# Weights of two feed-forward stages and the last attention's keys and values, prepared in steps inside the stage ahead

## The chip, the cores and the metric

The kernel runs on one core of one Trainium2 chip. The metric is the device time of one execution in microseconds (us); the number that counts is the median of repeated runs. The engines are PE (TensorE: matrix products, and transposes done as matrix products), DVE (VectorE), ACT (ScalarE), POOL (GpSimd) and SP (SyncE, which here issues the loads). "PEld" is PE's loading of the fixed operand, which overlaps its products. PSUM, the memory into which PE writes, is handed out in banks; every result has to be copied out of its bank by another engine before the bank can be used again.

## The reference

A network of four pairs of cross-attention and feed-forward stage on x (2048 tokens of 256 numbers), with a context of 1601 rows:

```python
x = x + _L0_xattn_ref(_layernorm(x, axis=-1), ctx_1024, ...)
x = x + _L0_ffn_ref(_layernorm(x, axis=-1), L0_ffn_gate_w, L0_ffn_experts)
x = x + _L1_xattn_ref(_layernorm(x, axis=-1), ctx_1024, mask_BxSxS2_ik0, L1_xattn_Wq, L1_xattn_Wk, L1_xattn_Wv)
x = x + _L1_ffn_ref(_layernorm(x, axis=-1), L1_ffn_fast_b, L1_ffn_w_fc, L1_ffn_w_proj, L1_ffn_u, L1_ffn_v, L1_ffn_gate)
x = x + _L2_xattn_ref(_layernorm(x, axis=-1), ctx_1024, L2_xattn_edge_index, ...)
x = x + _L2_ffn_ref(_layernorm(x, axis=-1), L2_ffn_w_up, L2_ffn_w_down)
x = x + _L3_xattn_ref(_layernorm(x, axis=-1), ctx_1024, ctx_1024, mask_1x1xSxS2_ik0, L3_xattn_Wq, ...)
x = x + _L3_ffn_ref(_layernorm(x, axis=-1), L3_ffn_w1, L3_ffn_b1, L3_ffn_w2, L3_ffn_b2)
```

What matters here are the two ternary feed-forwards. Their weights are turned into -1, 0 and 1 before they are used:

```python
# L1, "bitlinear": one scale for each row; a low-rank product is added to the first layer
scale = clip(mean(abs(w_latent), axis=1, keepdims=True), 1e-05, None)
tern  = clip(round(w_latent / scale), -1.0, 1.0)
h = x @ (tern * scale).T + gate * (x @ v.T @ fast_b.T @ u.T)
return bitlinear(maximum(h, 0.0) ** 2, w_proj)

# L2: one threshold for the whole matrix; the input is divided by its root mean square
alpha = mean(abs(w))
w_t = sign(w) * (abs(w) > 0.5 * alpha)
```

The last attention (L3) has 16 heads of 16 numbers, with a bias on queries, keys, values and output. The masks of L1 and L3 are such that only the last 400 rows of the context count; the kernel finds this out when it runs and then takes the branch described here.

## The kernel before

**Tiling.** x stays on the chip as 16 tiles of 128 tokens. A chunk is 512 tokens, four tiles, so each stage has four chunks (c = 0 to 3). The stages run one after another: attention 0, experts, a branch on what the masks hold, and then, in the branch that is taken, `attention1_tail` (L1, lines 883 to 992), `ffn1` (1028 to 1170), `attention1` (L2, 725 to 881), `ffn2` (1193 to 1279), `attention3_tail` (1500 to 1752) and `ffn3`.

**PSUM.** `banks` (line 88) opens three pools for a stage: two double banks for scores (`psc`), two banks for everything else (`pm`: transposes, projections, sums) and two accumulators (`pa`). A stage closes them at its end. `attention3_tail` opens 3, 1 and 1 for its main part.

**Attentions L1 and L2.** Before the first chunk they transpose their weights, make keys kT (and a rounded copy kb, line 923 in L1) and values v (lines 927 to 931). Then for each chunk come scores (974 to 977 in L1, 851 to 860 in L2), an exponential on ACT, and value products (984, 871) in four accumulations, one for each tile. What the next chunk needs (its norm, its queries q and qb, the maxima for the exponential) is written as a generator, `prepare`, and advanced by `step(nxt, n)` between the scores and between the accumulations: the helper takes n pieces of work from a generator, up to the next `yield`.

**ffn1.** It loads w_fc and w_proj (1 MB each) into raw weight buffers when the function is entered. Within the stage it then prepares: the absolute mean of each row (`scales`, the reduces of line 1054, DVE), the ternary weights (`ternary`, lines 994 to 1000: two DVE instructions, one for each comparison), their transposes in bf16 on PE with copies by ACT (`transpose_up` with 1009 and 1012, `transpose_down` with 1021 and 1025), and the low-rank matrices b4 and vh, vl from u, fast_b and v (1076 to 1104). Only then does the first chunk's norm follow (transposes of line 173, copies xnhi and xnlo of lines 179 and 180), with the low-rank product (1123), and the four chunks.

**ffn2.** The same for w_up and w_down, with one threshold for a matrix (`thresholds`: a reduce on DVE, and a product with ones, line 1214, to sum over partitions). Each chunk then has four pairs of score products (1245), gelu on ACT, a split in two parts (`parts`, 1172 to 1179), squares h * h on DVE (1256) with their sum on POOL (1257), and the down products (`down`, line 1186), two pairs late. At the end of a chunk PE sums the squares (1268) and DVE scales the result and adds it to x.

**attention3_tail.** It loads four weights, and prepares keys and values: transposed and padded weights (`transpose_weight`, lines 205 to 220, and 1574), keys in four groups (1582, 1586), values in four row blocks (1592). Its main part begins with the norm, the projection of the queries (1616 to 1621) and maxima.

**What sets the order.** In the attentions L1 and L2 and in the preparations a scheduler orders the instructions of each engine by their dependencies and the order in which they are written. In ffn1 and ffn2 PE's order is the written one from the start of the main part (`manual_schedule(engines={PE})`), and in the last attention's main part that of all engines. The raw weights of all stages share three buffers (`wraw`, 2048 numbers wide) in turn, so a load starts when the weights three earlier in the turn are no longer needed. All of them are issued by SP, in order.

Of the kernel before, what the change touches and what calls it, by code (L numbers as in the profile page):

```python
# [8 lines left out]
F32 = mybir.dt.float32  # L9
BF16 = mybir.dt.bfloat16  # L10
# [44 lines left out]
class Net:  # L55
# [44 lines left out]
    def psc(self):  # L100
        return self.ps_s.tile([P, 2, 512], F32, tag="s", name="psc")

# [102 lines left out]
    def transpose_weight(self, dst, raw, pad=None):  # L205

        nc = self.nc
        for kc in range(2):
            ps = self.pm()
            for o in range(2):  # L210
                nc.tensor.transpose(
                    ps[:, o * P : (o + 1) * P], raw[:, o, kc * P : (kc + 1) * P], self.ident
                )
            if pad:
                nc.scalar.copy(
                    dst[:, kc, :].rearrange("p (h e) -> p h e", e=32)[:, :, 0:16],
                    ps[:, :D].rearrange("p (h e) -> p h e", e=16),
                )
            else:
                nc.scalar.copy(dst[:, kc, :], ps[:, :D])  # L220

# [503 lines left out]
    def attention1(self, pre, mask=None, bias=False):  # L725
# [5 lines left out]
        with ExitStack() as s:  # L731
# [108 lines left out]
            for c in range(NCH):  # L840
# [25 lines left out]
                for i in range(TPC):  # L866
                    x = self.x[c * TPC + i]
                    acc = self.pa()
                    for kt in range(NKT):
# [5 lines left out]
                        if kt % 6 == 5:  # L875
                            step(nxt, 1)
                    ri = self.small.tile([P, 1], F32, name="ri1")
# [5 lines left out]
    def attention1_tail(self, pre, mask):  # L883
# [5 lines left out]
        with ExitStack() as s:  # L889
# [75 lines left out]
            for c in range(NCH):  # L965
# [14 lines left out]
                for i in range(TPC):  # L980
# [7 lines left out]
                    step(nxt, 1)  # L988
                    ri = self.small.tile([P, 1], F32, name="ri1")
# [12 lines left out]
    def transpose_up(self, dst, t):  # L1002

        nc = self.nc
        for kc in range(2):
            for j in range(2):
# [5 lines left out]
                nc.scalar.copy(dst[:, kc, j * 512 : (j + 1) * 512], ps)  # L1012

    def transpose_down(self, dst, t):

        nc = self.nc
        for f in range(0, 8, 2):
# [7 lines left out]
            nc.scalar.copy(dst[:, f : f + 2, :], ps.rearrange("p (k o) -> p k o", k=2))  # L1025


    def ffn1(self):
# [6 lines left out]
        self.load_rows("L1_ffn_w_proj", F, wpr)  # L1035
        with ExitStack() as s:
            self.banks(s)
            pool = s.enter_context(tc.tile_pool(name="f1", bufs=1))
            tp = s.enter_context(tc.tile_pool(name="f1t", bufs=3))
            hp = s.enter_context(tc.tile_pool(name="f1h", bufs=2))  # L1040
            u = pool.tile([P, NF, R], F32, name="u")
            vv = pool.tile([R, D], F32, name="vv")
            fb = pool.tile([R, R], F32, name="fb")
            gate = pool.tile([R, 1], F32, name="gate")
            nc.sync.dma_start(u, a["L1_ffn_u"].rearrange("(o p) r -> p o r", p=P))
            nc.sync.dma_start(vv, a["L1_ffn_v"])
            nc.sync.dma_start(fb, a["L1_ffn_fast_b"])
            nc.sync.dma_start(gate, a["L1_ffn_gate"].partition_broadcast(R))

            def scales(view, n, cols):  # L1050
                sc = pool.tile([P, n], F32, name=f"sc{n}")
                half = pool.tile([P, n], F32, name=f"half{n}")
                nhalf = pool.tile([P, n], F32, name=f"nhalf{n}")
                nc.vector.tensor_reduce(sc, view, AX.X, ALU.add, apply_absolute_value=True)
                nc.vector.tensor_scalar(sc, sc, 1.0 / cols, 1e-5, ALU.mult, ALU.max)
                nc.vector.tensor_scalar(half, sc, 0.5, None, ALU.mult)
                nc.vector.tensor_scalar(nhalf, sc, -0.5, None, ALU.mult)
                return sc, half, nhalf


            sc1, half, nhalf = scales(wfc, NF, D)
            rs1 = pool.tile([P, NF], F32, name="rs1")
            nc.vector.reciprocal(rs1, sc1)
            tfc = pool.tile([P, NF, D], BF16, name="tfc")
            for o in range(NF):
                self.ternary(tp, tfc[:, o, :], wfc[:, o, :], half[:, o : o + 1], nhalf[:, o : o + 1])
                nc.vector.tensor_scalar(u[:, o, :], u[:, o, :], rs1[:, o : o + 1], None, ALU.mult)
            wfT = pool.tile([P, 2, F], F32R, name="wfT")
            self.transpose_up(wfT, tfc)


            uT = pool.tile([R, F], F32, name="uT")
            b = pool.tile([R, F], F32, name="b")
            bh = pool.tile([R, 2, F], F32R, name="bh")
            b4 = pool.tile([P, F], F32R, name="b4")
            nc.gpsimd.memset(b4.bitcast(F32), 0.0)
            for j in range(2):
                ps = self.pm()
                for i in range(4):
                    nc.tensor.transpose(ps[0:R, i * P : (i + 1) * P], u[:, 4 * j + i, :], self.ident)  # L1080
                nc.scalar.copy(uT[:, j * 512 : (j + 1) * 512], ps[0:R, :])
                ps = self.pm()
                nc.tensor.matmul(ps[0:R, :], lhsT=fb, rhs=uT[:, j * 512 : (j + 1) * 512], start=True, stop=True)
                nc.vector.tensor_scalar(b[:, j * 512 : (j + 1) * 512], ps[0:R, :], gate, None, ALU.mult)
            nc.vector.tensor_copy(bh[:, 0, :], b)
            nc.vector.tensor_tensor(bh[:, 1, :], b, bh[:, 0, :].bitcast(F32), ALU.subtract)
            for k in range(4):
                nc.scalar.copy(b4[32 * k : 32 * k + R, :], bh[:, k % 2, :])

            v4 = pool.tile([P, 2, P], F32, name="v4")  # L1090
            nc.gpsimd.memset(v4, 0.0)
            vh = pool.tile([P, 2, P], F32R, name="vh")
            vl = pool.tile([P, 2, P], F32R, name="vl")
            ps = self.pm()
            for kc in range(2):
                nc.tensor.transpose(ps[:, kc * R : (kc + 1) * R], vv[:, kc * P : (kc + 1) * P], self.ident[:R, :R])
            for k in range(4):
                nc.vector.tensor_copy(
                    v4[:, :, 32 * k : 32 * k + R], ps[:, : 2 * R].rearrange("p (k r) -> p k r", k=2)
                )  # L1100
            nc.vector.tensor_copy(vh, v4)
            nc.vector.tensor_tensor(vl, v4, vh.bitcast(F32), ALU.subtract)
            sc2, half, nhalf = scales(wpr, 2, F)
            tpr = pool.tile([P, 2, F], BF16, name="tpr")
            for o in range(2):
                self.ternary(tp, tpr[:, o, :], wpr[:, o, :], half[:, o : o + 1], nhalf[:, o : o + 1])
            wpT = pool.tile([P, NF, D], F32R, name="wpT")
            self.transpose_down(wpT, tpr)

            scb = pool.tile([P, D], F32, name="scb")  # L1110
            ps = self.pm()
            for o in range(2):
                nc.tensor.transpose(
                    ps[:, o * P : (o + 1) * P], sc2[:, o : o + 1].to_broadcast([P, P]), self.ident
                )
            nc.scalar.copy(scb, ps[:, :D])
# [76 lines left out]
    def ffn2(self):  # L1193
# [7 lines left out]
        self.load_rows("L2_ffn_w_down", F, wdn)  # L1201
        with ExitStack() as s:
            self.banks(s)
            pool = s.enter_context(tc.tile_pool(name="f2", bufs=1))
            tp = s.enter_context(tc.tile_pool(name="f2t", bufs=3))
            hp = s.enter_context(tc.tile_pool(name="f2h", bufs=2))

            def thresholds(view, name):
                part = pool.tile([P, 1], F32, name=f"part{name}")
                half = pool.tile([P, 1], F32, name=f"half{name}")  # L1210
                nhalf = pool.tile([P, 1], F32, name=f"nhalf{name}")
                nc.vector.tensor_reduce(part, view, AX.XY, ALU.add, apply_absolute_value=True)
                ps = self.pm()
                nc.tensor.matmul(ps[:, 0:1], lhsT=self.ones, rhs=part, start=True, stop=True)
                nc.vector.tensor_scalar(half, ps[:, 0:1], 0.5 / (F * D), None, ALU.mult)
                nc.vector.tensor_scalar(nhalf, ps[:, 0:1], -0.5 / (F * D), None, ALU.mult)
                return half, nhalf

            half, nhalf = thresholds(wup, "u")
            tup = pool.tile([P, NF, D], BF16, name="tup")  # L1220
            tflat = tup.rearrange("p o i -> p (o i)")
            for o in range(0, NF, 4):
                self.ternary(tp, tflat[:, o * D : (o + 4) * D], wflat[:, o * D : (o + 4) * D], half, nhalf)
            half, nhalf = thresholds(wdn, "d")
            tdn = pool.tile([P, 2, F], BF16, name="tdn")
            for o in range(2):
                self.ternary(tp, tdn[:, o, :], wdn[:, o, :], half, nhalf)
            wuT = pool.tile([P, 2, F], F32R, name="wuT")
            self.transpose_up(wuT, tup)
            wdT = pool.tile([P, NF, D], F32R, name="wdT")  # L1230
# [4 lines left out]
            for c in range(NCH):  # L1235
# [4 lines left out]
                for f in range(0, NF, 2):  # L1240
# [20 lines left out]
                    if f == 2 and c + 1 < NCH:  # L1261
                        nxt = self.norm(c + 1, rms=True, split=hp)
# [603 lines left out]
```

## Time and profile before

| | us |
|---|---|
| median of 3 runs (2095.49 to 2098.01) | 2097.05 |
| the profiled execution | 2097.01 |
| its span, first to last instruction | 2095.2 |
| PE busy in it | 1866.5 (89%) |
| DVE busy | 1115.3 (53%) |
| ACT busy | 822.2 (39%) |
| POOL busy | 686.9 (33%) |

The mean granted clock of PE is 0.951 of full speed. The stages of the branch lie in the span as follows (us from its start): L1's attention from about 988 to 1101.7, ffn1 to about 1235, L2's attention to 1516.1, ffn2 to 1643.2, the last attention to about 1979, ffn3 to 2095.2.

In the rows of the profile, "PE pa L984" is an instruction of PE that writes a tile called pa and comes from line 984. A row of the chain of waits has its start and its length; where two rows don't touch, the time between them belongs to pieces of the chain that aren't shown. A busy PE isn't PE at its peak, since the ends of its products are modelled.

### The profile page before, as it was taken

To read this page: it belongs to the slowest core of one execution; us is meant where nothing else is said; L and a number is where in the kernel's file an instruction comes from. 1 tells how busy PE (TensorE), PEld (TensorE's weight loads), DVE (VectorE), ACT (ScalarE), POOL (GpSimd) and SP (SyncE) were. 2 spreads that over 40 slices of the span, in tenths; PEclk is the share of its full clock that TensorE was granted. 3 is DMA by queue.
4 is the path that set the end of the run, shared out by engine and by line. 5 is a ranking of instruction groups with operands and counts; after the bars stand their busy time and mean duration, and the time that the engine had idled before them with its cause. 6 is when DMAs were issued, how large, how long until landed. Compare 5 with 4: busy or idle time off the path is not lost.

```text
span 2095.2 us, 22283 instructions
## 1 busy us (share of the span) xinstructions
PE 1866.5 (89%) x8523; PEld 924.4 (44%) x8533; DVE 1115.3 (53%) x2170; ACT 822.2 (39%) x1121; POOL 686.9 (33%) x469
## 2 busy tenths in 40 slices
PE   7789999999999899886995899999968888988899
PEld 3233333333333443332453664555556522333487
DVE  4665565655644377778436643222176467766400
ACT  4554434434434247740113431111143256555432
POOL 1168878867868300028000120000033201111210
PEclk9799999999999799998997999999978889999999
DMA  8830000000000000001001000000000000000361
GB/s 285 280 100 1 1 1 1 1 1 0 1 1 1 1 1 1 1 1 63 8 0 43 1 23 1 0 1 0 0 1 1 6 1 1 1 1 1 130 194 61
DMA packets 39698, 63.49 MB, mean 30 GB/s; under 512 B 5133, under 2 KB 32158, under 8 KB 39582
## 3 DMA queue, kind: packets, MB, share of 16 engines
q1 hardware_dynamic: 37776, 60.33, 8.8%
q10 hardware_dynamic: 1806, 1.64, 0.2%
q8 instruction: 69, 1.13, 0.2%
q14 instruction: 47, 0.39, 0.1%
HBM read 59.87 MB, written 2.10 MB: 30 GB/s over the span
## 4 chain that ended last, share of the span: by engine, by line
PE 65%; DVE 15%; ACT 7%; issue 5%; POOL 5%; DMA 3%; SPq 0%; ACTq 0%; POOLq 0%; DVEq 0%
PE pa L468 7%; PE psc L456 5%; PE psc L851 5%; PE pa L871 4%; PE psc L1649 3%; DVE mp L381 3%; PE psc L1787 3%; PE pa L561 3%; PE pa L1798 3%; DVE ri L418 2%; ACT p L1656 2%; PE psc L454 2%; PE pm L1699 2%; PE pm L1616 2%; PE pm L376 2%
## 5 line engine op out<-in xcount | busy, mean ns | idle before, releaser
L477 POOL TENSOR_TENSOR sp<-sp,p 128x1024 f32<-128x1024 f32 (+1 forms) x176 | 418.7, 2379 | 56.9 <-ACT p L461 46.4
L381 DVE TENSOR_REDUCE mp<-pm 128x1 f32<-128x512 f32 x384 | 242.7, 679 | 160.2 <-PE pm L376 159.5
L461 ACT ACTIVATE p<-psc 128x1024 f32<-128x1024 f32 (+1 forms) x208 | 212.7, 1023 | 260.9 <-PE psc L456 162.2
L456 PE MATMUL psc<-qT,kT 64*128 64x512 f32 (+1 forms) x832 | 219.8, 591 | 0.0
L468 PE MATMUL pa<-p,v 128*64 128x512 f32 (+1 forms) x832 | 203.6, 611 | 0.0
L1656 ACT ACTIVATE p<-psc 100x1024 f32<-100x1024 f32 x128 | 124.0, 1021 | 76.1 <-PE psc L1649 72.5
L1635 DVE TENSOR_REDUCE ms<-psc 128x2 bf16<-128x800 f32 x128 | 122.7, 981 | 43.8 <-PE psc L1631 41.9
L144 POOL TENSOR_SCALAR rstd<-mv 128x4 f32<-128x4 f32 x32 | 8.7, 272 | 365.2 <-DVE mv L140 357.9
L376 PE MATMUL pm<-kb,qb 64*128 64x512 bf16 x384 | 100.3, 391 | 26.6 <-DVE mp L381 24.9
L468 PEld LDWEIGHTS pa<-p,v 128*64 128x64 f32 (+1 forms) x832 | 51.0, 137 | 132.4 <-issue 129.4
L851 PE MATMUL psc<-q,kT 128*128 128x512 f32 (+1 forms) x208 | 102.2, 610 | 0.0
L702 POOL TENSOR_SCALAR done<-done,g 128x256 f32<-128x256 f32 x32 | 32.4, 1013 | 205.3 <-DVE g L696 205.3
L657 DVE SCALAR_TENSOR_TENSOR ge<-bc,g,after 128x128 bf16<-128x128 f32 (+8 forms) x128 | 79.4, 648 | 33.7 <-ACT seen L642 25.3
L1691 POOL TENSOR_TENSOR attn<-o,ri 128x512 f32<-128x512 f32 x16 | 20.3, 1270 | 229.3 <-DVE ri L1689 208.1
L456 PEld LDWEIGHTS psc<-qT,kT 64*128 64x128 f32 (+1 forms) x832 | 85.4, 185 | 19.6 <-issue 6.3
L871 PE MATMUL pa<-v,p 128*128 128x257 f32 (+1 forms) x416 | 93.9, 381 | 0.2
L864 ACT ACTIVATE p<-psc 128x1024 f32<-128x1024 f32 (+1 forms) x28 | 26.9, 962 | 168.2 <-PE psc L860 168.2
L636 PE MATMUL psc<-ge,pick 128*8 128x512 bf16 (+3 forms) x332 | 75.5, 344 | 19.5 <-DVE ge L657 10.6
L454 PE MATMUL psc<-sh,negz 64*128 64x512 bf16 (+1 forms) x416 | 87.0, 384 | 3.3 <-ACT sh L403 3.2
L151 DVE TENSOR_SCALAR xn<-x,mv,rstd 128x256 f32<-128x256 f32 x128 | 51.6, 460 | 68.1 <-PE pm L173 66.8
L824 DVE TENSOR_REDUCE mp<-pm 128x1 f32<-128x512 f32 x64 | 34.3, 570 | 99.9 <-PE pm L819 90.6
L642 ACT ACTIVATE seen<-ge 128x1152 bf16<-128x1152 bf16 (+6 forms) x56 | 83.2, 1486 | 6.7 <-DVE ge L662 5.8
(354 smaller groups left out, 3382.3 us busy)
## 6 DMA issues: line engine op xcount, KB each, us to landing
w<-in_L_ffn_w_dram SPq DMA_DIRECT2D x16, 1024.0 KB, 7.0
head<-in_mask_BxSxS_ik_dram SPq DMA_DIRECT2D x16, 600.5 KB, 4.0
head<-in_mask_1x1xSxS_ik_dram SPq DMA_DIRECT2D x16, 600.5 KB, 4.2
tail<-in_mask_BxSxS_ik_dram SPq DMA_DIRECT2D x16, 200.0 KB, 4.1
tail<-in_mask_1x1xSxS_ik_dram SPq DMA_DIRECT2D x16, 200.0 KB, 4.1
x<-in_x_dram SPq DMA_DIRECT2D x16, 128.0 KB, 3.4
w_e<-in_L_ffn_experts_dram SPq DMA_DIRECT2D x2, 1024.0 KB, 7.4
out_dram<-y SPq DMA_DIRECT2D x16, 128.0 KB, 2.5
```

The source lines that it names most:

```text
L376: nc.tensor.matmul(pair[j][:, :wd], lhsT=qb[h, i * P : (i + 1) * P], rhs=kb[h, hp, k0 : k0 + wd], start=True, stop=True,)
L381: nc.vector.tensor_reduce(mp[:, i, j, n : n + 1], pair[j][:, :wd], AX.X, ALU.max)
L454: nc.tensor.matmul(sc[:r, j, :], lhsT=negz[h, :r], rhs=sh[h, :], start=True, stop=False)
L456: nc.tensor.matmul(sc[:r, j, :], lhsT=kT[h, hp, kt * P : kt * P + r], rhs=q[h, :], start=False, stop=True,)
L461: nc.scalar.activation(p[:r], sc[:r], AF.Exp, scale=DH**-0.5)
L468: nc.tensor.matmul(acc[h, :], lhsT=v[:r, kt, hp * P + h.start : hp * P + h.stop], rhs=p[:r, j, :], start=kt == 0, stop=kt == NKT - 1,)
L477: nc.gpsimd.tensor_tensor(sums[:r], sums[:r], p[:r], ALU.add)
L642: nc.scalar.activation(seen[:, (t + 1) * P :], ge[:, (t + 1) * P :], AF.Copy, accum_out=far[:, t, e : e + 1])
L851: nc.tensor.matmul(sc[:r, j, :], lhsT=kT[:, kc, ks], rhs=q[:, kc, :], start=kc == 0, stop=False)
L871: nc.tensor.matmul(acc[:, : D + 1], lhsT=p[:r, kt, i * P : (i + 1) * P], rhs=v[:r, kt, :], start=kt == 0, stop=kt == NKT - 1,)
L1635: nc.vector.tensor_reduce(ms[u % 2][:, i, 64 * k + DH : 64 * k + 64 : 32], ps[:, :, :NTAIL], AX.X, ALU.max)
L1656: nc.scalar.activation(p[:TR], sc[k][:TR], AF.Exp, scale=DH**-0.5)
```

## The change

`ffn1`, `ffn2` and `attention3_tail` are each split in two. The first half becomes a generator: `ffn1_weights`, `ffn2_weights` and `attention3_keys` hold the loads and all the preparation, with a `yield` after each piece. The second half is the main part. The generators are advanced within the stage ahead: `attention1_tail` takes two steps after each of its 16 accumulations, `attention1` (L2) one, and `ffn2` two after each of its 16 pairs of score products. `finish` runs what is left. The tiles of a preparation live in pools that are opened before those of the stage ahead, and the ternary helper has its own pool of two buffers (f1l, f2l). The values' weight wvT has a tile of its own.

The loads of ffn1's weights come ahead of those of L1's on SP, those of ffn2's ahead of L2's, and those of L3's at the start of ffn2; so the turn of the raw buffers changes too. The transposes' helpers yield after each evacuation.

```diff
+    def finish(self, steps):
+        with ExitStack() as s:
+            self.banks(s)
+            drain(steps)
...
-    def attention1(self, pre, mask=None, bias=False):
+    def attention1(self, pre, mask=None, bias=False, beside=None):
...
+                    step(beside, 1)
                     ri = self.small.tile([P, 1], F32, name="ri1")
...
-    def attention1_tail(self, pre, mask):
+    def attention1_tail(self, pre, mask, beside=None):
...
                     step(nxt, 1)
+                    step(beside, 2)
...
                 nc.scalar.copy(dst[:, kc, j * 512 : (j + 1) * 512], ps)
+                yield
...
-    def ffn1(self):
+    def ffn1_weights(self, s):
...
+        pool = s.enter_context(tc.tile_pool(name="f1", bufs=1))
+        tp = s.enter_context(tc.tile_pool(name="f1l", bufs=2))
+        u = pool.tile([P, NF, R], F32, name="u")
...
+        nc.sync.dma_start(u, a["L1_ffn_u"].rearrange("(o p) r -> p o r", p=P))
...
+        yield
...
+        for o in range(NF):
+            self.ternary(tp, tfc[:, o, :], wfc[:, o, :], half[:, o : o + 1], nhalf[:, o : o + 1])
+            nc.vector.tensor_scalar(u[:, o, :], u[:, o, :], rs1[:, o : o + 1], None, ALU.mult)
+            if o % 2:
+                yield
+        wfT = pool.tile([P, 2, F], F32R, name="wfT")
+        yield from self.transpose_up(wfT, tfc)
...
+        self.f1 = wfT, wpT, b4, vh, vl, sc1, scb
+
+    def ffn1(self):
+        tc, nc = self.tc, self.nc
+        NF = 8
+        wfT, wpT, b4, vh, vl, sc1, scb = self.f1
...
-    def ffn2(self):
+    def ffn2_weights(self, s):
...
+        half, nhalf = thresholds(wup, "u")
...
+        for o in range(0, NF, 4):
+            yield
+            self.ternary(tp, tflat[:, o * D : (o + 4) * D], wflat[:, o * D : (o + 4) * D], half, nhalf)
+        half, nhalf = thresholds(wdn, "d")
+        yield
...
+    def ffn2(self, beside=None):
...
                     if f == 2 and c + 1 < NCH:
                         nxt = self.norm(c + 1, rms=True, split=hp)
+                    step(beside, 2)
...
-    def attention3_tail(self, mask):
+    def attention3_keys(self, mask, s):
...
+        kv = s.enter_context(tc.tile_pool(name="kv3", bufs=1))
+        yield
...
+        wvT = kv.tile([P, 2, D], F32, name="wvT")
...
+        for w, n, pad in ((wkT, "Wk", True), (wqT, "Wq", True), (wvT, "Wv", None)):
+            yield from self.transpose_weight_steps(w, raw[n], pad)
...
+        for g in range(G):
+            ps = self.pm()
...
+            nc.scalar.activation(kT[:, g, :], ps[:, :NTAIL], AF.Identity, bias=kbias[:, g : g + 1])
+            nc.vector.tensor_copy(kb[:, g, :], kT[:, g, :])
+            yield
+        for kt in range(TK):
+            ps = self.pm()
...
+            yield
+        self.k3 = spread, qbias, bo, wqT, woT, kT, kb, v, ms
...
-        net.attention1_tail("L1_xattn", masks[0])
-        net.ffn1()
-        net.attention1("L2_xattn", bias=True)
-        net.ffn2()
-        net.attention3_tail(masks[1])
+        with ExitStack() as s1:
+            later = net.ffn1_weights(s1)
+            step(later, 1)
+            net.attention1_tail("L1_xattn", masks[0], later)
+            net.finish(later)
+            net.ffn1()
+        with ExitStack() as s2:
+            later = net.ffn2_weights(s2)
+            step(later, 1)
+            net.attention1("L2_xattn", bias=True, beside=later)
+            net.finish(later)
+            with ExitStack() as s3:
+                later = net.attention3_keys(masks[1], s3)
+                step(later, 1)
+                net.ffn2(later)
+                net.finish(later)
+                net.attention3_tail()
         net.ffn3()
```

The other branch, which isn't taken, runs the same halves one after the other.

## The prediction

> **What bounds the kernel now.** I read the stage sums first (busy time of each engine in a stretch), then the chain of waits at each of the three places from which the change takes work, then the list of waits in the second FFN. The columns of a stretch are its length, then PE, PEld, DVE, ACT and POOL busy with counts, the granted clock, DMA share and GB/s.
>
> ```profile
> 1101.70:1129.50 27.80, 12.17 (x48) 4.70 (x48) 20.39 (x51) 9.71 (x15) 3.29 (x4) 0.55 0.27 79
> 1516.10:1533.10 17.00, 5.47 (x37) 3.98 (x37) 14.75 (x19) 4.00 (x8) 4.78 (x5) 0.64 0.00 1
> 1643.20:1665.20 22.00, 20.52 (x70) 11.59 (x70) 5.80 (x22) 6.95 (x14) 3.82 (x5) 0.83 0.02 0
> ```
>
> These are the preparations of ffn1, of ffn2 and of the last attention. They are of two kinds. In the first two PE idles and DVE works; in the third PE itself is busy for 20.5 of 22 us, so that work isn't waiting, it is matrix work that must be done somewhere. The stages ahead of them, which are to take the work:
>
> ```profile
> 992.00:1101.70 109.70, 106.35 (x360) 55.60 (x360) 49.91 (x144) 18.20 (x27) 8.86 (x14) 0.95 0.04 15
> 1267.00:1516.00 249.00, 244.78 (x863) 136.81 (x871) 62.34 (x149) 37.25 (x50) 9.90 (x16) 1.00 0.00 0
> 1543.00:1644.00 101.00, 78.69 (x445) 69.25 (x444) 67.67 (x87) 35.58 (x51) 40.73 (x26) 0.88 0.01 3
> ```
>
> The two attentions are PE-bound (97% and 98%) with DVE at 46% and 25%: DVE work is free there, PE work is not. ffn2 is bound by no single engine. The chain of waits, last attention block into the first preparation:
>
> ```profile
> 1094.49 7.17 PE pa L984 x32
> 1101.77 2.29 DVE sc L1054
> 1104.53 2.19 DVE sc L1054
> ...
> 1129.54 1.34 PE pm L173 x5
> ```
>
> Its ends give the first hole: 1129.54 - 1101.7 = 27.8 us from the last value product to the transposes of ffn1's first norm. In the same way the second is 1516.08 to 1533.06, 17.0 us, and the third runs from the end of the sum products L1268 (1643.2) to the first maxima L1616 (1665.23), 22.0 us.
>
> How ffn2 waits from 1565 to 1644 (first what waits, then for what, total us, times, longest):
>
> ```profile
> POOL sq L1257 <- DVE h L1256: 24.4, 5, 9.9
> PE pm L1268 <- POOL sq L1257: 10.2, 3, 3.8
> PE pa L1186 <- DVE rlo L1178: 3.5, 3, 2.4
> ```
>
> A chunk takes 27 us, with PE busy for some 21 and DVE for some 19; its end is a chain DVE, POOL (2.35 us for each sq), PE, so extra DVE or ordered PE work is partly paid there.
>
> **What the Trainium skill says.** Trace Analysis, section Optimization Strategy: where a kernel has several regimes, interleaving them may pay. The rows above agree for the first two holes (DVE-led preparation beside a PE-bound stage) and less for the third. TensorE: Matmul & The Clock Gate, section What's actually happening: PE falls to half clock after an idle window of about 3.4 us. The granted clock of 0.55 and 0.64 in the first two holes, against 0.95 and 1.00 in the attentions, agrees. The same page, section Architectural detail, calls ACT and DVE strict FIFO; so a DVE instruction that is put early holds all behind it. The trace shows each engine's records in order; no run here tests it otherwise.
>
> **The change, part by part.** The profiled execution took 2097.01 us (span 2095.2), the median is 2097.05; so differences on the span carry over one to one. I give what each hole frees and then what comes back.
>
> *ffn1's weights, into the attention L1.* Freed: 27.8 us; after the last L984 PE goes straight to the norm's transposes. Paid:
> (a) The head of the attention. In the changed order DVE has w_fc's whole chain ahead of the first copy of kb: the reduce 2.29, five small ones about 0.4, eight ternary pairs of 0.345 + 0.476 = 6.6, together 9.3. Before, DVE reached that copy at 998.73, with the statistics of the norm done; so it falls to about 1008. Between the copies of kb, v, xn and qb then lie w_pr's reduce 2.28, its pairs 2 x (0.75 + 1.27) = 4.0 and u's scaling 1.8, in part where DVE idled (3.6 us for v, 3.5 for xn, 2.4 for qb). Those idle times hold about 6 of the 8 us, so 2 us are paid: the head is 11 to 12 us late. PE has nothing else there; it is bare.
> (b) Loads. SP now issues w_fc, w_pr and u ahead of L1's three weights, and u waits for the experts' pool (POOL's last add ends 988.2). I put Wk at about 994.5 and its use before at 989.1, 5.5 us late; it lies under (a), which is longer.
> (c) PE work put into a PE-bound stage: 32 bf16 transposes at 0.086 (the hole shows 0.134 at clock 0.64; scaled to full clock) 2.75, eight of u 1.1 (2.0 at 0.55), fb's products 2.1 (3.8 at 0.55), the rest 0.6: 6.6 us.
> (d) Stalls of PE on the two pm banks: each step evacuates by ACT (0.59 each) and the copies of b take 4.2 on ACT, ahead of which exponentials queue. No row shows this wait; at least 0, at most about 8 (the twelve evacuations one after another at 0.59 plus a wait); I take 3.
> Sum: -27.8 + 11.5 + 6.6 + 3 = -7. Bounds: -12 (head late by 7 only) to -2.
>
> *ffn2's weights, into the attention L2.* Freed: 17.0. Paid: 32 bf16 transposes and two threshold products, 3.2 us of PE in a stage with 4 us of slack in 249; the reduces (2 x 2.3) at about 1237 to 1253 under the transposes of L2's weights: 0; the ternary pairs (two of 0.7 + 1.28 for each matrix, 8 us of DVE) hold up chunk 0's maxima and shift: 2; a DVE copy of L1609 in the first chunk and pm stalls: 1. Sum: -17 + 6.2 = -10.8. Bounds -13 to -7.
>
> *The last attention's keys and values, into ffn2.* Freed: not all 22. After the change PE goes from the sum products to the norm of the last attention, and its transposes take the bank in which the last accumulator lay, which DVE frees only after the update of x (about 3 us later); with transposes, xnT, projection and qb it is some 6 us to the first maxima. Freed: 16. Paid: 20.5 us of PE at clock 0.83, about 14.3 at the clock of a busy ffn2, with two steps after each f, so all 18 within chunk 0 and the start of chunk 1. PE idles in a chunk for about 6 us, so 8 of 14 are bare if nothing else waits. But PE's order is fixed: a step's transposes wait for the bank, ACT's evacuation (0.59) and behind them stand the scores of the next f. I work chunk 0 out as +6.2, chunk 1 as +5.8 (norm of the next chunk behind a step, then L1586's kind of product behind xnlo), chunk 2 as +0.7: 12.7. Sum: -16 + 12.7 = -3. Bounds -9 to +4.
>
> *The rest.* Two small pools (f1l, f2l) and the changed turn of the three weight buffers: each load is issued earlier than its use by over 20 us except (b): 0. ffn3's first weights wait for the last attention's pools, as before: 0, at most 2 either way.
>
> Total: -7 - 10.8 - 3 = about -20 us: 2097 - 20 = 2077.
>
> **The rivals.**
> B, cover is better than I take it. For: DVE at half load in the attentions; PE's 22 us of idle in ffn2 are more than the 14 put in. Against: DVE's order at the head is in the program. Then the head costs 5, the stalls 0, ffn2 pays 5: -27.8 + 5 + 6.6 = -16; -17 + 3.2 = -13.8; -16 + 5 = -11; together -41: 2056.
> C, the gaps are closed but nearly given back: the head late by 16, stalls of 6 in the first attention (+0.5), ffn2's weights -8, and ffn2 longer by 18 (+2): -5.5: 2091. For: the fixed orders. Against: no wait on pm banks in the attentions' lists.
> D, slower. One mechanism, in ffn2: the two pm banks are shared by steps, norm and sums, and PE stands at each of the 18 steps until the one before is evacuated behind that engine's own queue (ACT's gelu of 1 us, DVE's h of 1.1, rlo). At 1.9 us a step ffn2 is 34 us longer and the third part +18, which just cancels the first two; at 2.2 us it is +24 and the kernel 2103. For: DVE and ACT waits in ffn2. Against: PE pm L173 waits there for 3.2 us in all over two times now.
> E, the scheduler leaves the work where it was: 2097. The order of the changed kernel's instructions shows it moved; nearly out.
>
> **How the numbers follow.** A 0.57 (2066 to 2088 by its bounds), B 0.13, C 0.18, D 0.07, E with any cancelling sum 0.05. A measurement can tell about 0.2%, 4.2 us, from no change. Faster: A, B and C, less C's edge, 0.87; same 0.06; slower 0.07. The range that leaves out no more than 2 in 10 goes from B's near half to C: 2057 to 2091.
>
> **What would show it.** After, the chain of waits runs from value products straight into L173's transposes after L1 and L2, with holes under 4 us. The first attention's first scores come 11 to 12 us later than 1010.99 counted from the experts' end; if 5 or less, B. ffn2 from its first scores to its last sum product lasts about 120 us against 108; over 140 is D. PE's busy total falls little (the same matrix work at a better clock), its idle time by about 15 us. The prediction is wrong if the first attention gains nothing, or ffn2 grows by over 25 us.

## The result and the profile after

The changed kernel takes 2074.81 us (median of four runs, 2074.35 to 2080.25); the kernel before took 2097.53 beside it (median of four, 2095.49 to 2101.64). The ratio is 0.9895, with a 95% interval from 0.9873 to 0.9917: 22.7 us less, where 20 were forecast. The profiled execution has a span of 2072.9 us, 22.3 less than before, so the trace accounts for the difference.

First the stages that took the work, in the changed kernel (length, then PE, PEld, DVE, ACT and POOL busy, granted clock, DMA share, GB/s): the head of attention L1, its main part, and ffn2 from its first scores to its last sum product.

```profile
988.50:1020.60 32.10, 18.91 (x53) 10.61 (x54) 29.00 (x87) 4.88 (x11) 5.27 (x9) 0.65 0.37 118
1020.60:1117.00 96.40, 96.07 (x371) 49.45 (x370) 42.74 (x114) 25.45 (x36) 5.06 (x8) 1.00 0.03 9
1510.60:1636.00 125.40, 100.13 (x531) 81.76 (x532) 74.20 (x114) 48.22 (x76) 43.93 (x30) 0.86 0.02 3
```

The same three stretches of the kernel before:

```profile
989.00:1010.80 21.80, 18.16 (x49) 10.46 (x50) 14.48 (x53) 4.87 (x11) 5.18 (x10) 0.70 0.36 128
1010.80:1101.70 90.90, 90.51 (x321) 46.56 (x319) 38.19 (x100) 15.27 (x21) 3.79 (x6) 1.00 0.00 1
1534.90:1643.20 108.30, 85.89 (x473) 74.59 (x473) 73.01 (x98) 42.90 (x64) 41.73 (x27) 0.88 0.01 3
```

Read length against busy. The head of L1 has grown by 10.3 us with PE's work unchanged and DVE's doubled: that is waiting. L1's main part has grown by 5.5 with PE busy for over 99.5% in both: that is work. In ffn2 PE's busy time rose by 14.2, and its idle time (length less busy) didn't fall but rose, from 22.4 to 25.3 us: on balance the work that was put in filled no gap.

Two of the three holes are gone, and the third is shorter. PE's own timeline of the changed kernel (start, length, idle time before it in brackets) at the ends of L1 and of L2, and at the end of ffn2:

```profile
1113.81 3.21 PE L997 MATMUL pa<-v,p 100*128 100x257 f32 x14
1116.86 1.04 PE L179 MATMUL pm<-ident,xn 128*128 128x128 f32 x8
...
1505.74 3.65 PE L882 MATMUL pa<-v,p 128*128 128x257 f32 x16
1509.23 1.04 PE L179 MATMUL pm<-ident,xn 128*128 128x128 f32 x8
...
1632.83 3.57 PE L1315 MATMUL pm<-ones,sq 128*128 128x1 f32 x16 [3.81 <-POOL sq L1303]
1640.03 1.08 PE L179 MATMUL pm<-ident,xn 128*128 128x128 f32 x4 [3.63 <-DVE x L1324]
1643.59 3.78 PE L1672 MATMUL pm<-xnT,w_l3q 128*128 128x512 f32 x4 [0.67 <-ACT xnT L183]
```

After L1 and L2 the value products run straight into ffn's transposes; after ffn2 7.2 us are left between the sums and the first projection, and that projection (four products) takes 3.78 us where it took 1.98.

A ledger from such marks, counted from POOL's last x of the experts (988.3 before, 987.8 after), so that what differs ahead of the change drops out:

| stretch | before | after | difference |
|---|---|---|---|
| head of L1, to its first scores | 22.5 | 32.8 | +10.3 |
| L1, first scores to last value product | 90.5 | 96.0 | +5.5 |
| to ffn1's first low-rank product (first hole) | 31.0 | 2.5 | -28.5 |
| ffn1 and the head of L2, to its first value product | 184.3 | 188.1 | +3.8 |
| L2, first to last value product | 199.1 | 201.8 | +2.7 |
| to ffn2's first scores (second hole) | 19.2 | 1.6 | -17.6 |
| ffn2, first scores to last sum product | 108.3 | 125.4 | +17.1 |
| to the first projection (third hole) | 22.0 | 7.6 | -14.4 |
| last attention and ffn3, to the end | 430.0 | 429.3 | -0.7 |
| sum | 1106.9 | 1085.1 | -21.8 |

Three questions were left for runs: what makes the head late, whether each part pays, and why ffn2 grows by more than the work put into it.

### The profile page after: what moved, and what is told of

Its sections match the earlier page's. It is cut to its first block, busy times and chain, and to the rows that moved or that the text cites. A ratio compares the mean times of both kernels' runs of the same rounds, so it can differ in the third digit from the quotient of the medians.

```text
span 2072.9 us, 22285 instructions
## 1 busy us (share of the span) xinstructions
PE 1853.8 (89%) x8533; PEld 915.1 (44%) x8533; DVE 1114.5 (54%) x2170; ACT 821.5 (40%) x1121; POOL 684.7 (33%) x469
## 5 line engine op out<-in xcount | busy, mean ns | idle before, releaser
L471 ACT ACTIVATE p<-psc 128x1024 f32<-128x1024 f32 (+1 forms) x208 | 212.7, 1023 | 260.5 <-PE psc L466 162.1
L1705 PE MATMUL psc<-q,kT 32*100 32x512 f32 x512 | 75.8, 641 | 10.4 <-ACT p L1712 10.0
L571 PE MATMUL pa<-w_e,xe 128*128 128x512 f32 x160 | 84.7, 655 | 0.0
## 6 DMA issues: line engine op xcount, KB each, us to landing
x<-in_x_dram SPq DMA_DIRECT2D x16, 128.0 KB, 3.6
out_dram<-y SPq DMA_DIRECT2D x16, 128.0 KB, 3.8
```

Of the source, the lines that this page charges most:

```text
L471: nc.scalar.activation(p[:r], sc[:r], AF.Exp, scale=DH**-0.5)
L1705: nc.tensor.matmul(sc[j // 2][:TR, j % 2, :], lhsT=kT[h, g, kt * TR : (kt + 1) * TR], rhs=q[u][h, :], start=True, stop=True,)
```

## The experiments

In different sessions the program reached the end of the experts, just before the changed code, anywhere from 986 to 994 us. Medians are given with their ratio to the kernel before of the same session (its medians were 2098.5 to 2100.4); for stages I count from the experts' end, where the changed kernel needs 1085.1 us to the end and the kernel before 1106.9. This count has a spread of its own: the stretch from the first projection of the last attention to the end, which no edit is aimed at, took anywhere from 427.4 to 431.7 us in the twelve traces. Where two totals differ by so little, only the stages that the edit touches are compared.

**One part undone at a time.** The generator is started, so loads and pools stay early, but it is only finished after the stage.

```diff
-            net.attention1_tail("L1_xattn", masks[0], later)
+            net.attention1_tail("L1_xattn", masks[0])
```

> ffn1's weights are not stepped inside attention L1, only finished after it; loads and pools stay early, so the scheduler still puts w_fc's DVE chain at the head of L1. Theory (the late head comes from the early pool and load, not from the steps): the head stays about 9 to 10 us late (first copy of kb near 1007), 5 us of PE work leave the attention, and after it a hole of about 14 us holds the transposes with their copies: about 2083 us. Rival (the steps hoist the DVE work): head back at its old place, hole of the full 28 us: about 2087 us. By the prediction's own sum the undone part is worth 7: 2082 us with the full hole.

2081.92 us, ratio 0.9922 (0.9890 to 0.9953); 1089.8 us from the experts' end. First copy of kb 19.8 us after the experts (19.9 in the changed kernel, 10.4 before), main part 5.1 us shorter, and 11.6 us from the last value product to the low-rank product. As the theory had it: the scheduler puts w_fc's work at L1's head whether or not it is stepped there, since it can start it; an early pool and an early load are enough. By the count from the experts' end stepping alone is worth 4.7 us, which is hardly more than that count's spread. From the experts' end to the low-rank product it is 133.9 us here, 131.3 to 132.8 in the traces of runs whose code is the changed kernel's up to there, and 144.0 before the change: most of this part's gain there comes without the steps.

```diff
-            net.attention1("L2_xattn", bias=True, beside=later)
+            net.attention1("L2_xattn", bias=True)
```

> ffn2's weights are finished after attention L2 and not stepped inside it. DVE's two reduces stay early (as the order shows), ternary pairs, transposes and copies come after. Theory: L2 gets 3 us shorter and a hole of about 13 us opens: about 2085 us. Prediction's sum (10.8 for the part): 2086 us. If below 2078, the part was worth nothing.

2080.65 us, ratio 0.9907 (0.9876 to 0.9937), some 4 us less than forecast; 1090.9 from the experts' end, 5.8 more than the changed kernel. Only 0.7 of these 5.8 lie in the stages that the edit touches: from L2's first value product to the first projection it is 337.1 us here and 336.4 in the changed kernel. So this part's steps are worth next to nothing as long as the keys are stepped in ffn2. L2 is 2.8 us shorter and 15.1 us lie between it and ffn2's scores, near the theory. What I hadn't expected: ffn2, which still has all 18 steps, takes 115.4 us here and not 125.4. PE's waits in ffn2, in this run:

```profile
PE pm L1315 <- POOL sq L1303: 9.6, 4, 3.8
...
PE pm L179 <- DVE xn L170: 1.4, 1, 1.4
```

and in the changed kernel:

```profile
PE pm L179 <- DVE xn L170: 11.3, 3, 8.1
PE pm L1315 <- POOL sq L1303: 9.4, 3, 3.8
```

In e2 the second chunk's normalized x is made at the end of the hole (1528.85 to 1530.22), and ACT does all four of that norm's sums of squares ahead of its first gelu. In the changed kernel ACT does two of the four (L167) behind gelu and the first split:

```profile
1515.03 1.02 ACT L1296 ACTIVATE h<-psc 128x1024 f32<-128x1024 f32 x1
...
1517.14 1.04 ACT L1296 ACTIVATE h<-psc 128x1024 f32<-128x1024 f32 x1
1518.06 0.43 ACT L167 ACTIVATE sq<-xn 128x256 bf16<-128x256 f32 x1
...
1519.39 0.43 ACT L167 ACTIVATE sq<-xn 128x256 bf16<-128x256 f32 x1
```

and PE, whose order is written, stands 8.1 us before that norm's transposes with later scores behind them. So some 10 of the 17.6 us that the second hole gave are paid again within ffn2. The next run shows that the closed hole alone doesn't cause that wait.

```diff
-                net.ffn2(later)
+                net.ffn2()
```

> The last attention's keys and values are finished after ffn2 and not stepped inside it. Theory from the marks (ffn2 grew by 17 us, the hole after it fell by 12.6): about 2070 us, faster than the changed kernel by 4 to 5. The prediction's sum (the part gains 3): 2078 us. ffn2 from its first scores to its last sum product should be 109 to 111 us again.

2078.68 us, ratio 0.9896 (0.9864 to 0.9928), the same ratio as the changed kernel; 1087.3 from the experts' end. My theory fell: ffn2 took 112.5 us and not 109 to 111, and the hole behind it 21.1. From ffn2's first scores to the first projection it is 133.6 us against 133.0 with the steps. Stepping the keys within ffn2, as the change does it, is worth nothing: what the hole gives, the stage loses.

The run also says more about e2. Its second hole is closed too (1.6 us), yet ACT does all four sums of the second chunk's norm ahead of gelu (they end at 1522.61, gelu starts at 1523.99), and PE's waits for that norm stay short:

```profile
PE pm L179 <- DVE xn L170: 3.5, 2, 2.2
```

The wait of 8.1 us thus needs both, the closed hole and a step behind the first scores; together they change the order that the scheduler makes for ACT. Why it chooses that order wasn't traced. Set side by side, with e4 from below:

| run | second hole | keys' steps in ffn2 | ffn2 | L2's first value product to the first projection |
|---|---|---|---|---|
| before | 19.2 | none | 108.3 | 348.6 |
| e2 | 15.1 | among the scores | 115.4 | 337.1 |
| e3 | 1.6 | none | 112.5 | 337.0 |
| changed kernel | 1.6 | among the scores | 125.4 | 336.4 |
| e4 | 1.6 | at the chunk ends | 113.7 | 324.6 |

Each of the two parts alone gains some 11.5 us. Both together, as the change has them, gain 12.2; with the steps at the chunk ends they gain 24.0.

**Other places for the steps in ffn2.**

```diff
                         nxt = self.norm(c + 1, rms=True, split=hp)
-                    step(beside, 2)
                 for f, parts in late:
                     self.down(acc, f, parts, wdT, NF)
+                step(beside, 5)
```

> The 18 steps of the last attention's keys run five at a time at the end of each chunk of ffn2, between the last down products and the products that sum the squares, where PE waits 3.8 us for POOL's sum, and no longer ahead of the next chunk's norm. Theory (the 17 us came from PE's written order, which puts steps ahead of the norm and the scores): ffn2 grows by about 5 instead of 17: about 2062 us. Rival (the work itself has no room in ffn2, by the two pm banks and ACT): ffn2 still grows by 12 or more: 2070 us or above.

2064.34 us, ratio 0.9841 (0.9809 to 0.9873); 1072.2 from the experts' end, 12.9 less than the changed kernel (11.8 of them from ffn2's first scores to the first projection). ffn2 takes 113.7 us, 5.4 more than before the change, as forecast. Its stretch:

```profile
1510.90:1624.60 113.70, 96.91 (x531) 79.54 (x532) 79.21 (x115) 48.21 (x76) 44.73 (x30) 0.91 0.01 3
```

The same 531 products as in the changed kernel, but PE idles for 16.8 us and not 25.3, and the clock is higher. PE's wait for POOL's sums at the chunk ends:

```profile
PE pm L1268 <- POOL sq L1257: 14.0, 4, 3.8
...
PE pm L1315 <- POOL sq L1303: 4.5, 2, 2.4
```

The first row is of the kernel before, the second of this run. The changed kernel had 9.4 there, so the place at the wait accounts for about 5 us of its difference to e4; 7 come from the norm, for which PE waits 4.2 us in all here and 11.3 there, and other waits take some of it back (those for rlo are 5.2 us and not 1.5).

```diff
                         nxt = self.norm(c + 1, rms=True, split=hp)
-                    step(beside, 2)
+                    if f:
+                        step(beside, 2)
```

> As the changed kernel, but no step of the last attention's keys after the first pair of scores of a chunk of ffn2: two steps after each of the other three pairs, so none is written ahead of the next chunk's norm. Theory one (steps ahead of the norm are what cost): ffn2 grows by about 9 us instead of 17: 2067 us. Theory two (any step among the scores costs, for PE's order puts it ahead of products that were ready): ffn2 still grows by 14 us or more: 2072 us or above.

2074.97 us, ratio 0.9886 (0.9863 to 0.9909); ffn2 124.5 us. Theory one fell, theory two stands: it isn't only steps ahead of the norm that cost. Without them the wait of 8.1 us is gone (the longest for that norm is 2.2), but other waits come in its place. PE's timeline of this run:

```profile
1521.30 1.04 PE L179 MATMUL pm<-ident,xn 128*128 128x128 f32 x8
1526.55 0.66 PE L220 MATMUL pm<-ident,w_l 128*128 128x128 f32 x2 [4.21 <-issue]
```

Now the norm is in time, 9 us after the first scores, but it holds both pm banks until DVE has made xnlo (the first of the two ends at 1526.45), and the step behind it stands for 4.2 us. That the bank is what it waits for is read from that coincidence; the row names no releaser.

**The head of L1.**

```diff
+            s.enter_context(tc.manual_schedule(engines={mybir.EngineType.DVE}))
             made = []
             drain(prepare(0, made))
```

> Only VectorE's order in attention L1's main part is changed: it is the written one, so w_fc's chain comes after the first scores and not ahead of the first copy of kb. Theory (the late head is VectorE's order): from the end of the experts to the first scores 25 us or less instead of 32.8 (22.5 before the change), the rest of it being the late load of Wk; about 8 us faster than the changed kernel, 2067 us. Rival (the late load of Wk sets the head): still 31 us or more, no gain.

2079.23 us, ratio 0.9911 (0.9888 to 0.9934). The head is as short as before the change (first scores after 22.9 us), though Wk's load is still late: its transposes start 5.9 us after the experts' end, where before the change they started 1.2 us ahead of it. So the late load alone doesn't make the head late; VectorE's order does. But nothing is won: the main part takes 107.3 us and not 96.0, since the written order puts whole chains of ternary work ahead of L1's own norm and updates there. PE idles for 7.4 us in it and not 0.3, and the same 371 products take it 4.3 us longer, at a clock of 0.97 and not 1.00. Its longest waits:

```profile
PE pm L179 <- DVE xn L157: 2.7, 3, 1.9
PE pa L998 <- DVE x L1006: 1.9, 1, 1.9
```

The forecast of 2067 was a miss: I had counted the head and not what comes after it.

```diff
             self.load_rows(f"{pre}_{n}", D, raw[n])
+        step(beside, 1)
...
             later = net.ffn1_weights(s1)
-            step(later, 1)
             net.attention1_tail("L1_xattn", masks[0], later)
```

> Only the order of the loads is changed: attention L1's three weights are issued ahead of w_fc and w_proj, as before the change; VectorE's order is left to the scheduler. Theory: Wk's transposes start about 5 us earlier, but the first copy of kb still waits behind w_fc's chain, so the first scores move by 2 us at most: about 2073 us. Rival (load order sets the head): first scores 5 us or more earlier, 2070 us or less.

2068.44 us, ratio 0.9857 (0.9836 to 0.9878). First scores after 24.3 us, 8.5 earlier, and L1 ends 6.9 earlier. The measured gain is that of the rival, but not by its mechanism alone. In the changed kernel PE waited twice at the head:

```profile
PE pm L220 <- DMA w_L_xattn<-in_L_xattn_Wk_dram: 11.0, 1, 11.0
PE pm L940 <- DVE kb L936: 7.3, 2, 6.6
```

Here it is 3.7 and 5.5. With w_fc loaded later the scheduler also reckons with later data and puts only the reduce ahead of kb, and the ternary pairs one by one into DVE's waits:

```profile
996.47 2.27 DVE L1071 TENSOR_REDUCE sc<-w_fc 128x8 f32<-128x2048 f32 x1
...
998.65 1.05 DVE L937 CAST kb<-pm 128x400 bf16<-128x400 f32 x2
...
1001.34 0.42 DVE L945 COPY v<-pm 100x256 f32<-100x256 f32 x1 [0.90 <-PE pm L941]
1001.68 0.48 DVE L1015 SCALAR_TENSOR_TENSOR tfc<-w_fc,half,lo 128x256 bf16<-128x256 f32 x1
```

So the load order matters twice, once on the queue and once through the order that the scheduler makes of it. How the 8.5 us divide between the two wasn't tried; with VectorE's order written in both, the loads first are worth 4.9 us at the head (22.9 in e5, 18.0 in e8 below).

**Joined.** All three edits as shown above (e5's written order, e6's loads first, e4's steps at the ends):

> Joined: VectorE in the written order in attention L1, L1's loads first, and the steps of the last attention's keys at the chunk ends of ffn2. Theory (the causes are separate and add): first scores of L1 about 10 us earlier than in the changed kernel and ffn2 12 us shorter: about 2052 us. If what is won at the head comes back within L1 (PE bound there), 2060 us.

2059.08 us, ratio 0.9806 (0.9781 to 0.9831). The first scores come after 18.0 us, the best of all, but L1 ends after 128.0, about as late as in the changed kernel (128.8): what the written order wins at the head it loses in the main part. So the forecast of 2052 fell, and its alternative of 2060 held. Without the written order, e6's edit and e4's alone:

> Joined: L1's loads first (VectorE's order left to the scheduler) and the steps of the last attention's keys at the chunk ends of ffn2. If the two gains of these edits alone add, counted from the end of the experts (5 and 13 us below the changed kernel's 1085 us): 1067 us from there to the end, and a median near 2056 us. If the second gives back part of the first, 1072 us or more.

2054.40 us, ratio 0.9796 (0.9778 to 0.9815), 1066.2 us from the experts' end: the two gains add, and this version is faster than both kernels, by 2% against the kernel before. Last, the steps of the last chunk after its sum products:

```diff
-                step(beside, 5)
+                if c + 1 < NCH:
+                    step(beside, 5)
...
                 nc.vector.tensor_copy(ss, ps[:, :TPC])
+                if c + 1 == NCH:
+                    step(beside, 5)
```

> As the run before it, but the steps that are left for the last chunk of ffn2 (three value products) run after the products that sum the squares, while PE waits 3.5 us for the update of x. Theory (that wait also lets the clock fall, so that the first projection of the last attention takes 3.78 us instead of 2.0): filled, the first projection starts within 0.5 us of its old time after the sums, takes about 2 us, and the kernel gains 2 to 3 us. Rival (the first projection is slow for another reason): no gain, within 1 us.

2056.69 us, ratio 0.9803 (0.9786 to 0.9819), so no gain; the theory fell. Stretches of this run, at the late steps, the norm and the first projection:

```profile
1616.60:1620.30 3.70, 3.65 (x9) 2.06 (x8) 1.56 (x6) 0.00 (x0) 1.21 (x2) 0.50 0.00 0
1620.30:1624.20 3.90, 1.31 (x8) 0.84 (x8) 1.20 (x3) 1.17 (x2) 0.00 (x0) 0.94 0.00 0
1624.20:1627.80 3.60, 3.59 (x4) 1.18 (x4) 0.00 (x0) 0.00 (x0) 0.00 (x0) 0.54 0.00 0
```

The filled wait did bring the clock back, from 0.50 to 0.94. But the norm behind it keeps PE busy for only 1.31 of 3.9 us, and for the projection the clock is at 0.54 again (3.62 us). The slow projection is a matter of the clock (its four products take 1.98 us at a granted clock of 1.00 before the change, 3.78 at 0.50 in the changed kernel), but one filled wait isn't enough. The Trainium skill (TensorE: Matmul & The Clock Gate, section What's actually happening) puts the fall after an idle window of about 3.4 us; here 3.9 us in which PE was busy for a third were followed by it.

## Why the prediction was right, and where its steps weren't

The sum, -20, was right to 2.7 us. That is partly luck: by the ledger one of its three terms was met, and the other two were off by 5.7 us each, in opposite directions.

- *ffn1's weights*, forecast -7, measured -12.7 (10.3 + 5.5 - 28.5), just outside its bounds of -12 to -2. Step (a), the late head behind w_fc's chain, was 10.3 against 11 to 12, with kb at the time that was worked out (1007.7 for "about 1008"), and e5 shows it to be DVE's order. Calling it "bare" was right for the head. Step (b), the late load "under (a)", was wrong as a cause: e6 wins 6.9 us by the load order, partly because DVE's order hangs on it. Step (c), PE work, was 5.5 against 6.6. Step (d) is the one that failed: 3 us of stalls on pm banks were taken, and PE idled for 0.3 us in the whole main part.
- *ffn2's weights*, forecast -10.8. From ffn1's start to ffn2's first scores it is 3.8 + 2.7 - 17.6 = -11.1. But L2 itself grew by 2.7 and not 6.2, and 3.8 were lost in ffn1 and the head of L2, where I had put nothing. Some 1.4 of these 3.8 are ffn1's same 476 products, which keep PE busy for 87.6 us and not 86.1, at a clock of 0.92 and not 0.95; the rest was not traced to a cause, and e2 to e10, with the same code there, need 2.4 to 5.3 us more than before. And a cost was missing that falls later: with this hole closed, the keys' steps make ffn2 10 us longer than with it open (e2), so that undoing this part alone costs only 0.7 us.
- *Keys and values*, forecast -3, bounds -9 to +4; measured +17.1 - 14.4 = +2.7. The failed step is the price of ffn2, 12.7 against 17.1. Counted from one chunk's sum products to the next (from the first scores for the first chunk), the first chunk grew by 10.9 us (forecast 6.2), the second by 6.6 (5.8) and the third by -0.5 (0.7): what was missed lies in the first, where PE stands for 8.1 us before a norm that the scheduler's order made late; no term of the prediction names that order. I had taken 6 us of idle time a chunk as room for PE work, "if nothing else waits". The stretches show that on balance none of it was filled; e4 shows that room was there, at the chunk ends, and e3 that the part as written is worth nothing beside the closed second hole. The slow first projection, 1.8 us by the profile, wasn't in the forecast. Two lines of the working are also wrong, with little bearing on the sum: 20.5 us at a clock of 0.83 are 17.0 at full clock and not 14.3 (they hold the norm's transposes, which stay; PE's busy time did rise by 14.2), and at eight steps a chunk the 18 reach into the third chunk (the last value product of the keys' part starts at 1586.5, the second chunk's sums at 1581.1). L1616, called the first maxima, is the first projection.
- *The rest*, forecast 0: -0.7, and -0.5 ahead of the change.

Of the rivals, B (2056) had its mechanism in reach: e9 reaches 2054 once the loads are in their old order and the steps at the chunk ends (head 1.9 us later than before the change, ffn2 5.4 longer). D, ffn2 slower by 34 us, had the stage and PE's written order right, but the steps cost about 1 us apiece, 17.1 over 18, and not 1.9, and the longest wait is for the norm and not for a bank. Of the signs, the first two holes came under 4 us, the first scores 10.3 us later for 11 to 12, and ffn2 took 125.4 us for about 120. PE's idle time fell by less than the 15 us forecast: 1866.5 busy of 2095.2 before and 1853.8 of 2072.9 after leave 9.6 us less.

## What to carry to other kernels

An engine's idle time is no room by itself where its order is written. Here the same steps left PE idle in ffn2 for 25.3 us when they stood among the scores, and for 16.8 when they stood at the chunk ends, where it waits. Undo parts of a change singly and together: two parts that meet in one stage each gained some 11.5 us alone and 12.2 as a pair, and only another place for the steps brought the 24. Where a scheduler orders by when data is expected, the order of the loads is an order of the engines as well: e6 moved only the loads, with the opening of their pools, and VectorE's order moved with them.

## What the runs showed of the hardware

Four scalings of xn on DVE took 1.14 us in the kernel before. In the changed kernel, beside a sum on POOL, they took 3.22; the first two rows are of the changed kernel:

```profile
1523.16 3.22 DVE L170 TENSOR_SCALAR xn<-xn,rmsi 128x256 f32<-128x256 f32 x4
1523.32 2.38 POOL L1303 TENSOR_TENSOR sq<-sq,h 128x1024 f32<-128x1024 f32 x1 [1.41 <-DVE h L1302]
```

```profile
1539.52 1.14 DVE L164 TENSOR_SCALAR xn<-xn,rmsi 128x256 f32<-128x256 f32 x4
```

Of the sixteen such scalings in the changed kernel the median took 0.346 us and the longest 2.434. The longest is the second of these four, the only one of the sixteen beside a sum of POOL: it starts at 1523.42 and ends at 1525.85, just after the sum (1525.70). That DVE waits for POOL there is likely from this; no run here tests it by itself. PE waits 1.8 us more for it, behind the 8.1 us above, between the first of that norm's eight transposes and the other seven.
